# One of GpSimd's six block differences per chunk pair, done by an accumulating DMA inside SBUF

## The chip, the cores and the metric

The kernel runs on one core of one Trainium2 chip. The metric is the device time of one execution in microseconds. Three runs of the kernel before the change gave 461.73, 461.80 and 462.26 us; their median is 461.8 us. A profiled execution of the same kernel took 462.24 us, of which the profile's span covers 460.4 us. Times inside the profile are counted from the start of that span.

## The reference

The kernel computes a compressed interaction network over a batch of 1024 rows, with 64 fields and an embedding of 16. Three layers multiply every field of the input with every field of the running state, contract the products with a weight matrix, and add a bias. Half of each of the first two layers goes to the output and half to the next layer.

```
for i in range(3):
    z = jnp.einsum('bfe,bge->bfge', x0, h).reshape(B, f0 * fh, e)
    y = jnp.einsum('oc,bce->boe', Ws[i], z) + bs[i][None, :, None]
    if i != 2:
        x_i, h = y[:, :64, :], y[:, 64:, :]
    else:
        x_i, h = y, y
    xs.append(x_i)
return jnp.sum(jnp.concatenate(xs, axis=1), axis=2) @ fc_w.T + fc_b
```

All of it is fp32.

## The kernel before, in words

The batch is cut into 32 chunks of 32 rows. A chunk's columns are 32 rows times 16 embedding values, so N = 512. The products of two copies of the input are symmetric, so a chunk needs 16 product tiles of 128 x 512; four of them form a block `z`, 128 x 2048 fp32, 1 MB. Fourteen such blocks live in SBUF, and `take()` and `used()` hand them out and get them back in the order in which they came free.

Six chunks at the head and tail are done plainly. The other 26 form 13 pairs, and a pair (one chunk called `a`, one called `b`) is done with seven block multiplications in place of eight, in the manner of Strassen and Winograd. For that, sums and differences of product blocks and of weight blocks are needed. Per pair:

- VectorE makes the product blocks X (of chunk a), B22, T3 and B21, in two blocks each that the code tells apart by j = 0 and j = 1 (`w_product` L630, printed by the profile as `z<-xa,xp` at L632).
- GpSimd makes six differences, `w_mix` L641, printed as `z<-z,z` at L647. With j = 0 the whole block of four tiles is taken (128x2048), with j = 1 only three of the four (128x1536). The six are, in this order: T2 = T3 - X for j = 0 and j = 1; T3 = B22 - T2 for j = 0 and j = 1, in place; T2 = T2 - B21 for j = 0 and j = 1, in place. The last two are called the final T2 here.
- TensorE multiplies these blocks with weights and with sums of weights (`ws`, of five parts s1, s2, s3, s4 and neg) and collects the results in the PSUM tiles alpha, beta and delta. All of it is printed at L524, the helper `mm`. A weight is 128 x 64, so a multiplication fills half of TensorE's columns; the two halves run side by side.

The weights `ws` are made once at the head by `w_sums` (L774): GpSimd makes s1 to s3, ScalarE writes s4 = -h and neg.

The order is written by hand. Every job is put down with a time, `at(when, ...)`, in units of one slot, and at the end all jobs are issued in the order of these times (L994). The times decide only the order on each engine's queue; what an engine waits for is worked out from the tiles that it reads and writes. `window` (L729) lays out one pair's multiplications as two columns, one for each half of TensorE, and `zipped` interleaves them. The first column has 7 jobs on X, a few that fill up from the pair before, 7 on T2 (`w_run(p, alpha, s2, "T2")`), fill again, and 7 on T3 with s1. The second column has 7 on T3 with s3, 10 left over from the pair before, 7 on B21, and then the jobs on the final T2 (`w_run(p, delta, neg, "T2")`), of which one or two are left to the next pair's window (`second_fill`, L710). So T2 is read twice: first in its first form at jobs 10 to 16 of the first column, then in its final form from job 24 of the second column. The first pair of the 13 differs (L848 to L853): its window has fewer jobs, T2 in its first form is jobs 9 to 15 of the first column, the final T2 starts at place 20 of the second column, where three of the places before it are empty, and one of its B21 blocks is made by GpSimd.

Loads of the next pair are put down by `load_pair` (L755) and issued by SyncE: `xa` (1 MB each, L144), four `xb` of 256 KB (L158), `e` and `xx` (128 KB each, L162 and L167).

In the lists of `make_pair` (L679) the first ten times are those of the products, the six of `mixed` those of the differences: -14, -6.9, 7.2, 12.4, 16.4, 21.7 for the first pair and -5, 2.8, 7.2, 12.4, 16.4, 21.7 for the others.

Of the kernel before, what the change touches and what calls it, by code (L numbers as in the profile page):

```python
# [38 lines left out]
AF = mybir.ActivationFunctionType  # L39
ALU = mybir.AluOpType  # L40
# [10 lines left out]
NI = 4  # L51
# [17 lines left out]
def cin_kernel(ctx, tc, xra, xrb, wh, w0r, w1h, w2t, wx1, wx0, vec, out):  # L69
    nc = tc.nc  # L70
# [8 lines left out]
    def const_tile(name, shape):  # L79
        return const.tile(shape, F32, tag=name, name=name)  # L80

    blocks = [const_tile(f"z{n}", [128, NI, N]) for n in range(NZ)]
    vacant, left = list(range(NZ)), {}

    def take(uses=1):
        n = vacant.pop(0)
        left[n] = uses
        return n

    def used(n, times=1):  # L90
        left[n] -= times
        assert left[n] >= 0
        if left[n] == 0:
            vacant.append(n)
# [22 lines left out]
    for base in (0, 64, -64):  # L117
        nc.gpsimd.affine_select(
            out=shift, in_=shift, compare_op=ALU.not_equal, fill=1.0, base=base,
# [11 lines left out]
    ws = const_tile("ws", [128, 5, 2 * NI, F])  # L131
# [275 lines left out]
    def m_ap(f1, f2, dims):  # L407
        return bass.AP(tensor=md.tensor, offset=md.offset + f1 * row + f2 * F, ap=dims)
# [3 lines left out]
    for half, queue in enumerate((nc.sync, nc.scalar)):  # L412
        queue.dma_start(
            out=m_ap(0, 32 * half, [[row, F], [1, 32 * F]]), in_=m_rows[halves[half]]
# [5 lines left out]
        out=m_ap(64, 68, [[row, 4], [4 * F, 7], [1, 4 * F]]),  # L420
        in_=m_rows[0:4, 4 * F :].rearrange("p (k c) -> p k c", c=4 * F),
# [92 lines left out]
    def at(when, fn, *args, **flags):  # L514
        ops.append((when, len(ops), fn, args, flags))

    def zipped(when, *columns):
        for n, column in enumerate(columns):
            for m, job in enumerate(column):
                if job is not None:  # L520
                    at(when + m + n / len(columns), *job)
# [99 lines left out]
    def w_run(p, out, w, name, start=False, at_t=0, order=GROUPS):  # L621
        return [
            (w_job, p, out, w, j * NI + i + at_t, name, start and n == 0)
            for n, (j, i) in enumerate(order)
        ]

    wh_all, wq_all = w_all[:, :, 0:64], w_all[:, :, 64:128]
    s1, s2, s3, s4, neg = (ws[:, n] for n in range(5))
# [12 lines left out]
    def w_mix(p, j, out, in0, in1):  # L641
        p.setdefault(out, {})
        if j not in p[out]:
            p[out][j] = p["X"][j] if j and p["k"] > 3 else take(9 - 2 * j)
        o, x, y = p[out][j], p[in0][j], p[in1][j]
        tiles = slice(j, NI)
        nc.gpsimd.tensor_tensor(  # L647
            blocks[o][:, tiles], blocks[x][:, tiles], blocks[y][:, tiles], ALU.subtract
        )
        for b in (x, y):  # L650
            if b != o:
                used(b)
# [26 lines left out]
    def make_pair(t, p, when, mixed):  # L679
        a, b = p["a"], p["b"]  # L680
        for when, c, j, name, uses in (
            (when[0], b, 2, "B22", 5), (when[1], b, 0, None, 0), (when[2], b, 0, "T3", 9),
            (when[3], a, 0, "X", 5), (when[4], b, 3, "B22", 6), (when[5], b, 1, None, 0),
            (when[6], b, 1, "T3", 9), (when[7], a, 1, "X", 12 if p["k"] > 3 else 6), (when[8], a, 2, "B21", 5),
            (when[9], a, 3, "B21", 6),
        ):
            if name is None:
                at(t + when, w_both, p, j)
                continue
            if name == "B21" and j == 2 and p["k"] == 3:  # L690
                at(t + when, w_product, p, c, j, name, uses, engine=nc.gpsimd)
                continue
            if name != "T3":
                at(t + when - (3.3 if p["k"] > 4 and name == "B22" and j == 2 else 2.7), second, c, j)
            at(t + when, w_product, p, c, j, name, uses)
        for when, j, *names in zip(
            mixed, (0, 1, 0, 1, 0, 1), *zip(
                *(2 * (("T2", "T3", "X"),) + 2 * (("T3", "B22", "T2"),) + 2 * (("T2", "T2", "B21"),))
            )
        ):  # L700
            at(t + when, w_mix, p, j, *names)

    def first_fill(p):
        a = p["a"]
        return [
            (w_job, p, beta, wq_all, NI, "X"), (w_job, p, beta, wq_all, NT - NI, "B21"),
            (lambda: q_extra(a, va, p["beta"]),),
        ]

    def second_fill(p):  # L710
        return [
            (w_job, p, delta, wh_all, NI, "X"), (w_job, p, delta, wh_all, NT - NI, "B21"),
        ] + w_run(p, delta, neg, "T2")[7 - p["late"] :]

    def left_run(p, out, start=False):
        return [(w_job, p, out, neg, NI, "T3", start), (w_job, p, out, s4, NI, "B22")]
# [1 line left out]
    def late_run(p, left=True):  # L718
        b = p["b"]
        return (left_run(p, alpha) if left else []) + w_run(p, alpha, s4, "B22") + [(lambda: q_extra(b, vb, p["alpha"]),)]  # L720
# [8 lines left out]
    def window(t, p, fill, late, pad=[], order=GROUPS[4:] + GROUPS[:4]):  # L729
        zipped(  # L730
            t,
            w_run(p, alpha, wq_all, "X", True, order=order) + fill[0] + w_run(p, alpha, s2, "T2")
            + fill[1] + w_run(p, alpha, s1, "T3")
            + [(w_job, p, alpha, wh_all, NI, "T3"), (w_job, p, alpha, s1, NI, "B22")],
            w_run(p, delta, s3, "T3", True) + late
            + w_run(p, beta, wq_all, "B21", True, 2 * NI)
            + pad + w_run(p, delta, neg, "T2")[: 7 - p["late"]],
        )
        at(t + 30.2, squares, p)
        at(t + 6.8, snap_p1, p)  # L740
        at(t + 6.9, snap_p7, p)
        at(t + 6.8 + len(fill[0]) + 7, snap_u2, p)

    def end_pair(t, p, whens):
        hb_, qa, uub, ha, uua, xv, add = whens
        at(t + hb_, w_hb, p)
        at(t + qa, w_qa, p)
        at(t + uub, w_uu, p, alpha, "A", snaps[2])
        at(t + ha, w_ha, p)
        at(t + uua, w_uu, p, delta, "O", snaps[0])  # L750
        at(t + xv, x_v0x, p["k"])
        at(t + add, sums, p["k"])


    def load_pair(t, p, b0, a0, b1, a1):  # L755
        a, b = p["a"], p["b"]
        at(t + b0, load_xa, b)
        at(t + b0, load_xb, b, 2, 0)
        at(t + a0, load_xa, a)
        at(t + a0, load_xb, a, 0)  # L760
        at(t + b1, load_xb, b, 3, 1)
        at(t + a1, load_xb, a, 1, 2, 3)
        for c in (b, a):
            at(t + 1, load_e, c)
            at(t + 14, square, c)
        at(t + 1.1, load_xx, p["k"])
# [7 lines left out]
    def w_sums(m):  # L774
        h, q = w_all[:, 8 * m : 8 * m + 8, 0:64], w_all[:, 8 * m : 8 * m + 8, 64:128]
        if m:
            nc.gpsimd.tensor_tensor(ws[:, 3], q, ws[:, 1], ALU.subtract)
            nc.gpsimd.tensor_tensor(vb[halves[1]], va[halves[1]], w0ds[halves[1]], ALU.subtract)
            nc.scalar.activation(ws[:, 4], h, AF.Identity, scale=-1.0)
            nc.scalar.activation(ws[:, 4, NI], ws[:, 2, NI], AF.Identity, scale=-1.0)  # L780
            return
        nc.gpsimd.tensor_tensor(ws[:, 2], h, q, ALU.subtract)
        nc.gpsimd.tensor_tensor(ws[:, 1], ws[:, 0], q, ALU.add)
# [49 lines left out]
    for n in range(NPAIR):  # L833
        k = n + 3
        s = k % 2
        p = {
            "k": k, "A": halves[s], "O": halves[1 - s], "b": 2 * k + s, "a": 2 * k + 1 - s,
            "late": 1 + n % 2 if n else 0,
        }
        pairs.append(p)  # L840
        t = T0 + SPAN * n
        if n == 0:
            load_pair(t, p, -39.9, -33.3, -33.15, -27)
            make_pair(
                t, p, (-23.4, -20.7, -20.4, -17.8, -17.2, -16.8, -16.6, -7, -13.5, 3),
                (-14, -6.9, 7.2, 12.4, 16.4, 21.7),
            )
            left5 = [[(contract_half, 5, 3, i, n) for i in (2, 3)] for n in range(2)]  # L848
            window(
                t, p, ([left5[1][0], (q_extra, 4, va)], [left5[1][1]]),  # L850
                [left5[0][0], (q_extra, 5, va), None, None], [left5[0][1], None],
                GROUPS,
            )  # L853
        else:
            q = pairs[-2]
            load_pair(t, p, -34, -28, -27.8, -27.7)
            make_pair(
                t, p, (-21.4, -18.7, -18.4, -15.8, -12.2, -9.5, -6.1, -2, 1.6, 4.2),
                (-5, 2.8, 7.2, 12.4, 16.4, 21.7),
            )  # L860
            window(t, p, (first_fill(q), second_fill(q)), late_run(q))
            end_pair(t, q, (0.7, 11.7, 17.9, 22.3, 23.2, 24, 27.5))
# [220 lines left out]
```

## Time and profile before

| what | value |
|---|---|
| median of three runs | 461.8 us |
| profiled execution | 462.24 us |
| its span | 460.4 us |
| TensorE's granted clock over the span | 1.00 |
| VectorE busy | 394.0 us, 86% |
| ScalarE busy | 117.1 us, 25% |
| GpSimd busy | 367.7 us, 80% |
| the 78 differences of GpSimd | 310.4 us, 4019 ns each on the mean |
| one difference of 128x2048, of 128x1536 | 4.55 us, 3.46 us |
| one product block on VectorE | 2280 ns |
| DMA, all queues | 86.04 MB, 187 GB/s on the mean |

A group line of the profile gives the line of the program, the engine, the operation, what is written and read, the shapes and the count; then the busy time and the mean duration of one; then the idle time of the engine just before them and what ended most of it. In a timeline line the first number is the start, the second the duration, both in us. PE is TensorE, PEld its weight loads, DVE VectorE, ACT ScalarE, POOL GpSimd and SP SyncE. An fp32 multiplication shows as two instructions.

### The profile page before, as it was taken

How to read it: one execution, taken by the hardware profiler on the slowest of the kernel's cores; microseconds unless marked ns; L12 is line 12 of the kernel's file. 1: busy time of each engine (PE TensorE's matmuls, PEld its weight loads, DVE VectorE, ACT ScalarE, POOL GpSimd, SP SyncE). 2: the span in 40 equal slices, each digit the busy share in tenths (PEclk: the TensorE clock that was granted, in tenths of full speed). 3: DMA queues.
4: the chain of work that ended last, by engine and by line, in shares of the span. 5: the costliest groups of instructions: out<-in, count | busy, mean ns of one | idle time of the engine just before them, and what ended most of it. 6: DMA issues, size and time to landing. Idle time of an engine off the chain costs nothing.

```text
span 460.4 us, 6106 instructions
## 1 busy us (share of the span) xinstructions
PE 453.5 (99%) x2328; PEld 166.5 (36%) x2328; DVE 394.0 (86%) x284; ACT 117.1 (25%) x216; POOL 367.7 (80%) x112
## 2 busy tenths in 40 slices
PE   7999999999999999999999999999999999999997
PEld 4565343343333333333333333333333333333335
DVE  3995599899898989989898998989899998979551
ACT  2162250241313123131213213131311313124011
POOL 5323688998998979899798979989798989989800
DMA  8996998393728173663818264481827448240000
GB/s 295 417 297 149 324 407 321 130 323 111 270 86 319 30 260 140 188 212 131 282 35 290 100 233 166 135 277 48 304 73 250 161 163 279 79 149 18 22 0 2
DMA packets 32613, 86.04 MB, mean 187 GB/s; under 512 B 6116, under 2 KB 6788, under 8 KB 27656
## 3 DMA queue, kind: packets, MB, share of 16 engines
q1 hardware_dynamic: 31800, 84.70, 53.4%
q10 hardware_dynamic: 784, 0.95, 0.8%
q8 instruction: 18, 0.29, 0.3%
q14 instruction: 11, 0.09, 0.1%
HBM read 84.00 MB, written 1.64 MB: 186 GB/s over the span
## 4 chain that ended last, share of the span: by engine, by line
PE 82%; DMA 7%; DVE 3%; SPq 2%; POOL 2%; ACT 1%; issue 1%; POOLq 0%; DVEq 0%
PE alpha L524 57%; PE delta L524 9%; PE beta L524 7%; PE q L524 3%; DMA z<-in_wx 3%; PE acc L250 2%; DMA xa<-in_xra 2%; DVE z L632 2%; DMA xb<-in_xrb 1%; DMA md<-z 1%; SPq L457 1%; POOL z L240 1%; POOL z L535 1%; PE misc L113 1%; PE xp L219 1%
## 5 line engine op out<-in xcount | busy, mean ns | idle before, releaser
L647 POOL TENSOR_TENSOR z<-z,z 128x2048 f32<-128x2048 f32 x78 | 310.4, 4019 | 31.3 <-PE alpha L524 31.3
L632 DVE TENSOR_TENSOR z<-xa,xp 128x2048 f32<-128x2048 f32 x103 | 232.6, 2280 | 16.2 <-POOL z L647 13.1
L524 PE MATMUL alpha<-z,ws 128*64 128x512 f32 x624 | 211.6, 592 | 0.6 <-DVE alpha L943 0.6
L524 PE MATMUL delta<-z,ws 128*64 128x512 f32 x364 | 163.1, 594 | 0.0
L524 PEld LDWEIGHTS alpha<-z,ws 128*64 128x64 f32 x624 | 66.4, 137 | 113.5 <-issue 110.7
L524 PE MATMUL beta<-z,w_all 128*64 128x512 f32 x234 | 105.0, 593 | 0.0
L552 ACT COPY xp<-xb 128x512 f32<-128x512 f32 x88 | 51.6, 588 | 204.8 <-DVE z L632 181.3
L524 PE MATMUL alpha<-z,w_all 128*64 128x512 f32 x208 | 94.2, 595 | 1.1 <-DVE uu L288 0.7
L524 PEld LDWEIGHTS delta<-z,ws 128*64 128x64 f32 x364 | 48.6, 137 | 13.6 <-issue 11.2
L240 DVE TENSOR_TENSOR z<-xa,xp 128x2048 f32<-128x2048 f32 (+2 forms) x23 | 45.1, 2003 | 9.6 <-ACT xp L552 8.2
L524 PEld LDWEIGHTS alpha<-z,w_all 128*64 128x64 f32 x208 | 27.4, 137 | 61.1 <-issue 48.0
L240 POOL TENSOR_TENSOR z<-xa,xb 128x2048 f32<-128x2048 f32 x6 | 27.2, 4557 | 20.6 <-DMA xb<-in_xrb 20.6
L524 PEld LDWEIGHTS beta<-z,w_all 128*64 128x64 f32 x234 | 31.4, 137 | 14.6 <-issue 14.5
L250 PE MATMUL acc<-z,w_all 128*64 128x256 f32 x256 | 29.1, 382 | 1.6 <-DVE z L240 1.4
L524 PE MATMUL acc<-z,w_all 128*64 128x512 f32 (+1 forms) x96 | 30.0, 594 | 0.0
L524 PE MATMUL delta<-z,w_all 128*64 128x512 f32 x52 | 24.6, 593 | 0.0
L250 PEld LDWEIGHTS acc<-z,w_all 128*64 128x64 f32 x256 | 18.0, 137 | 13.8 <-DVE z L240 3.1
L292 DVE TENSOR_REDUCE acc<-uu 128x64 f32<-128x1024 f32 (+2 forms) x19 | 19.6, 1035 | 0.2
L638 DVE TENSOR_TENSOR xp<-xp,xb 128x512 f32<-128x512 f32 x26 | 18.2, 699 | 0.8
L655 ACT COPY snap<-alpha 64x512 f32<-64x512 f32 x13 | 7.6, 581 | 41.7 <-PE delta L524 34.2
L524 PE MATMUL y<-e,v 64*64 64x512 f32 x64 | 17.0, 613 | 0.0
L524 PE MATMUL q<-z,w_all 128*64 128x384 f32 (+1 forms) x128 | 16.9, 381 | 0.0
(117 smaller groups left out, 322.5 us busy)
## 6 DMA issues: line engine op xcount, KB each, us to landing
xa<-in_xra SPq DMA_DIRECT2D x32, 1024.0 KB, 4.7
xb<-in_xrb SPq DMA_DIRECT2D x128, 256.0 KB, 6.8
e<-in_xra SPq DMA_DIRECT2D x28, 128.0 KB, 4.5
xx<-in_xra SPq DMA_DIRECT2D x28, 128.0 KB, 2.5
z<-in_w2t SPq DMA_DIRECT2D x2, 1024.0 KB
z<-in_wx SPq DMA_DIRECT2D x2, 1024.0 KB, 9.2
z<-in_w1h SPq DMA_DIRECT2D x1, 1024.0 KB
xa<-in_xra SPq DMA_DIRECT2D x3, 256.0 KB
```

The source lines that it names most:

```text
L113: nc.tensor.matmul(misc[:, 0:n], zeros, zeros[:, 0:n], start=True, stop=True)
L219: nc.tensor.matmul(xbs[c][j][halves[h]], shift[halves[r], at : at + F], xas[c][halves[r], 0, :], start=True, stop=True,)
L240: engine.tensor_tensor(blocks[zs[c, j]][:, at, :], xas[c][:, at, :], xbs[c][j].unsqueeze(1).to_broadcast([128, last - first, N]), ALU.mult,)
L250: nc.tensor.matmul(accs[c][halves[n]], w_all[:, t, 0:64], blocks[zs[c, j]][:, i, n * H2 : (n + 1) * H2], start=(t == 0), stop=(j == last a ...
L292: nc.vector.tensor_reduce(acc[rows, of, k, half], uu[rows, of if at is None else at, E * half.start : E * half.stop].rearrange("p k (b e) ...
L457: queue.dma_start(out=ms[halves[half], 1, j * NI : (j + 1) * NI], in_=skewed(0, 16 * half + 4 * (j + 1), [[row, NI], [1, F]]),)
L524: nc.tensor.matmul(out, w, rhs, start=start, stop=stop, skip_group_check=True)
L552: nc.scalar.copy(bank, xbs[c][j])
L632: engine.tensor_tensor(blocks[b], xas[c], xbs[c][j].unsqueeze(1).to_broadcast([128, NI, N]), ALU.mult)
L638: nc.vector.tensor_tensor(bank, bank, xbs[p["b"]][j], ALU.add)
L647: nc.gpsimd.tensor_tensor(blocks[o][:, tiles], blocks[x][:, tiles], blocks[y][:, tiles], ALU.subtract)
L655: nc.scalar.copy(snaps[0][p["O"]], alpha(p))
```

## The change

The final T2 of j = 0 is no longer a GpSimd operation. GpSimd issues a DMA that reads block B21 and adds it into block T2, both in SBUF. A DMA of this kind adds[...]. So the signs are turned: T2 is now X - T3, T3 becomes B22 + T2, and the final T2 is T2 + B21. To make up for it, s2 (`ws[:, 1]`), which multiplies the first T2, is negated in place at the head by one more ScalarE instruction, after GpSimd has used the old value for s4's part `ws[:, 3]`; and the final T2 is multiplied with the plain weights `wh_all` (tiles 8 to 15) where it was multiplied with `neg`. The other five differences stay on GpSimd.

The order on GpSimd's queue changes as well. It was: T2 j0, T2 j1, T3 j0, T3 j1, final T2 j0, final T2 j1. Now it is: T2 j0, T2 j1, T3 j0, the DMA for the final T2 j0, T3 j1, final T2 j1. The number of TensorE's and VectorE's instructions and their order stay as they were.

```diff
@@ w_mix
-        nc.gpsimd.tensor_tensor(
-            blocks[o][:, tiles], blocks[x][:, tiles], blocks[y][:, tiles], ALU.subtract
-        )
+        if in1 == "B21" and j == 0:
+            nc.gpsimd.dma_start(out=blocks[o], in_=blocks[y], accum_op=ALU.add)
+        else:
+            nc.gpsimd.tensor_tensor(
+                blocks[o][:, tiles], blocks[x][:, tiles], blocks[y][:, tiles],
+                ALU.subtract if in1 == "T3" else ALU.add,
+            )
@@ make_pair
-                *(2 * (("T2", "T3", "X"),) + 2 * (("T3", "B22", "T2"),) + 2 * (("T2", "T2", "B21"),))
+                *(2 * (("T2", "X", "T3"),) + 2 * (("T3", "B22", "T2"),) + 2 * (("T2", "T2", "B21"),))
+    def p4_run(p):
+        return w_run(p, delta, wh_all, "T2", at_t=2 * NI)
@@ second_fill
-        ] + w_run(p, delta, neg, "T2")[7 - p["late"] :]
+        ] + p4_run(p)[7 - p["late"] :]
@@ window
-            + pad + w_run(p, delta, neg, "T2")[: 7 - p["late"]],
+            + pad + p4_run(p)[: 7 - p["late"]],
@@ w_sums
+            nc.scalar.activation(ws[:, 1], ws[:, 1], AF.Identity, scale=-1.0)
             nc.scalar.activation(ws[:, 4], h, AF.Identity, scale=-1.0)
@@ the times of the differences, first pair and others
-                (-14, -6.9, 7.2, 12.4, 16.4, 21.7),
+                (-14, -6.9, 7.2, 14.2, 14.1, 18),
-                (-5, 2.8, 7.2, 12.4, 16.4, 21.7),
+                (-5, 2.8, 7.2, 14.2, 14.1, 18),
```

## The prediction

> **What bounds the kernel now.** I read the busy shares first, then the chain of work that ended last, then one steady pair on the timeline.
>
> ```profile
> PE 453.5 (99%) x2328; PEld 166.5 (36%) x2328; DVE 394.0 (86%) x284; ACT 117.1 (25%) x216; POOL 367.7 (80%) x112
> PE 82%; DMA 7%; DVE 3%; SPq 2%; POOL 2%; ACT 1%; issue 1%; POOLq 0%; DVEq 0%
> ```
>
> TensorE is busy for 453.5 of 460.4 us and is 82% of the chain; GpSimd is 2% of it. A busy TensorE need not be at its peak, so I looked at its steps. In a steady pair (the window that starts at 244.72) two matmuls, one for each column half, start every 0.43 us without a hole. The change leaves their number alone, so there is nothing to win there. Time can only be lost, where a block comes too late for TensorE. The block in question is the final T2 of j = 0. GpSimd makes it now:
>
> ```profile
> 251.02 4.56 POOL L647 TENSOR_TENSOR z<-z,z 128x2048 f32<-128x2048 f32 x1
> 255.54 3.48 POOL L647 TENSOR_TENSOR z<-z,z 128x1536 f32<-128x1536 f32 x1
> 258.97 4.55 POOL L647 TENSOR_TENSOR z<-z,z 128x2048 f32<-128x2048 f32 x1
> 263.49 3.44 POOL L647 TENSOR_TENSOR z<-z,z 128x1536 f32<-128x1536 f32 x1
> ```
>
> These are T3 j0, T3 j1, final T2 j0, final T2 j1. TensorE's rows on both sides:
>
> ```profile
> 252.92 0.59 PE L524 MATMUL beta<-e,va 128*64 128x512 f32 x1
> ...
> 264.95 0.59 PE L524 MATMUL beta<-z,w_all 128*64 128x512 f32 x1
> 265.37 0.59 PE L524 MATMUL alpha<-z,ws 128*64 128x512 f32 x1
> 265.38 0.59 PE L524 MATMUL delta<-z,ws 128*64 128x512 f32 x1
> ```
>
> The first row ends the fill ahead of the T2 jobs. T2 j0's eight instructions follow at 0.4265 us each, so the last starts at 252.92 + 8 x 0.4265 = 256.33 and ends at 256.92: only then may T2 j0 be overwritten. The last row is the first reader of the final T2. The **budget in a steady pair** is 265.33 - 256.97 = 8.4 us (0.04 us off each end for the signal). GpSimd's own version ends at 263.52, 1.9 us early.
>
> The first pair is tighter:
>
> ```profile
> 97.85 0.59 PE L524 MATMUL alpha<-z,ws 128*64 128x512 f32 x1
> 100.42 4.54 POOL L647 TENSOR_TENSOR z<-z,z 128x2048 f32<-128x2048 f32 x1
> 103.62 1.88 PE L524 MATMUL alpha<-z,ws 128*64 128x512 f32 x4
> 105.01 0.64 PE L524 MATMUL delta<-z,ws 128*64 128x512 f32 x1
> ```
>
> T2 j0 is released at 97.85 + 0.59 = 98.44. GpSimd finished the final T2 at 104.96 and TensorE took it at 105.01, 0.1 us after its previous matmul (104.91). The **budget in the first pair** is 104.92 - 98.48 = 6.4 us, with no slack at all.
>
> Last, the DMA engines in the two budgets (the last two numbers of a row are DMA share and GB/s):
>
> ```profile
> 257.00:265.40 8.40, 8.40 (x42) 2.76 (x40) 8.18 (x9) 1.87 (x3) 8.40 (x3) 1.00 0.07 23
> 98.00:100.00 2.00, 2.00 (x13) 0.67 (x9) 1.97 (x2) 0.00 (x0) 2.00 (x1) 1.00 0.97 409
> 100.00:102.00 2.00, 1.99 (x10) 0.61 (x9) 2.00 (x2) 0.92 (x2) 2.00 (x2) 1.00 1.05 340
> 102.00:104.00 2.00, 2.00 (x9) 0.70 (x9) 2.00 (x2) 0.96 (x3) 2.00 (x1) 1.00 0.85 164
> ```
>
> and the page's row of a plain 1 MB load (issue to landing, us):
>
> ```profile
> xa<-in_xra SPq DMA_DIRECT2D x32, 1024.0 KB, 4.7
> ```
>
> In the steady pair they stand idle just then; in the first pair loads fill them until 104.
>
> [...]
>
> **The change, part by part.**
>
> *The transfer in a steady pair.* No row of before shows an adding transfer. `xa` moves as many bytes: at the 409 GB/s of the full engines 1.049 MB takes 2.56 us, so 4.7 - 2.56 = 2.1 us are fixed. [...] Lower end, the add at a copy's rate: 2.5 + 2.56 = 5.1 us. Upper end, two reads and the write one after the other: 2.5 + 3 x 2.56 = 10.2. I take two reads with the write beside them: 2.5 + 5.1 = 7.6 us, and 0.3 us for a 128 KB `e` load that shares the stretch (131 KB / 409): 7.9. That is under 8.4 with 0.5 us to spare: hidden, 12 pairs, 0 us. If the cover is gone, every us of lateness costs 12 us.
>
> *The transfer in the first pair.* The loads after 98.5 are 409 x 1.5 + 340 x 2 + 164 x 2 = 1.62 MB. [...] I take the middle, **2.7 us, once**.
>
> *GpSimd's queue.* The DMA instruction stands ahead of T3 j1 and waits for TensorE. In the steady pair GpSimd is free at 255.58, waits until 256.97[...], so T3 j1 runs 258.0 to 261.5 in place of 255.5 to 259.0. Its reader comes after the four T3 j0 jobs that start at 262.79, at 266.2: 4.7 us of cover. Final T2 j1 then ends at 265.0, where it ended at 266.93; its reader is at 265.38 + 4 x 0.853 = 268.8. In the first pair T3 j1 ends at about 103, its reader is at 105.34 + delay. 0 us. GpSimd saves 3.5 us a pair off the path.
>
> *VectorE.* The block B21 j0 comes free only when the transfer lands, and a later product takes it. In a steady pair that product starts 23.8 us into the window (242.40 - 218.6), the landing is at 20.6: 0. In the first pair it is the product at 107.83, which would slip to 109.1; the X product that follows ends 2 x 2.28 later, at 113.7, and TensorE, 2.7 us late, wants it at 114.9. 0.
>
> *ScalarE at the head.* One more 128x512 pass, 0.63 us by L779, and the group now waits for GpSimd's L777 (ends 58.0; L779 began at 58.06 anyway). The copy behind it slips by 0.6 us, VectorE's next product by 0.2; VectorE then waits 0.58 us for GpSimd at 80.14. 0; without that cover, 0.2.
>
> *Weights `wh_all` for `neg`:* same shapes, 0.
>
> Sum: 462.24 + 2.7 = 464.9 for an execution like the profiled one, which lies 0.44 above the median; on the median 461.8 + 2.7 = **464.5 us**.
>
> **The rivals.** (1) *The transfer is late in every pair.* For it: only 0.5 us of slack on an operation no row shows. At the upper end, 10.5 us with the `e` load, it costs 12 x 2.1 = 25 us; half-way, 12 x 1.0 + 3.5 = 15.5, so **477**. It decides from 8.4 us on. (2) *No change, the other side:* in the first pair the sum lands within 6.4 us. That needs an add at a copy's rate which gets past the loads[...]; **462.0**. Against it: the second read. (3) *Faster, a freer GpSimd speeds VectorE.* TensorE starts every second window 0.11 us late on a VectorE product that ends at 244.67; six of these are 0.7 us, so at best **461.1**, within 0.2%. Against it: VectorE's product takes 2.28 us with GpSimd busy or idle beside it. That the change doesn't do what it says can be left out: the built order of instructions shows 13 DMAs in place of 13 differences.
>
> **Numbers.** 0.2% (0.9 us) is about what a measurement of this kernel can tell from no change. Chances: forecast 0.42, (1) 0.37, (2) 0.16, (3) 0.05. Of these, slower by over 0.2% are nearly all of the first two, 0.79; same 0.17; faster 0.04. The forecast's own range is 463.0 to 466.5 (1.2 to 4.2 late). The range 461.8 to 484 leaves out the faster case, part of (2), and the worst of (1).
>
> **What would show it.** Right: TensorE's one new hole near 105, 1 to 4 us, ended by a DMA `z<-z`; none in later pairs; landing about 8 us after the issue. Wrong: a hole at the same place of every window (rival 1), or none (rival 2). GpSimd should fall to about 367.7 - 13 x 3.5 = 322 us. An adding transfer slower than two reads would break the forecast most.

## The result and the profile after

The changed kernel takes 468.8 us where the kernel before takes 462.0 on the same chip: a ratio of 1.0147 with a 95% interval of [1.0130, 1.0165], so 6.8 us more. The forecast was 464.5. The profiled execution of the changed kernel took 468.71 us, with a span of 466.9.

The page of the changed kernel: busy times, the clock granted to TensorE in 40 slices, the software queue (the one that GpSimd's DMA uses: packets, MB, share of 16 engines), the chain of work, GpSimd's group of differences, and the row of the adding transfer (KB each, us from issue to landing).

```profile
PE 455.7 (98%) x2328; PEld 166.7 (36%) x2328; DVE 393.8 (84%) x284; ACT 117.4 (25%) x217; POOL 321.7 (69%) x112
PEclk9999999997999999999999999999999999999999
q0 software_dynamic: 1872, 13.63, 15.1%
PE 78%; DMA 12%; SPq 3%; DVE 2%; issue 1%; ACT 1%; POOL 1%; POOLq 0%; DVEq 0%; ACTq 0%
L650 POOL TENSOR_TENSOR z<-z,z 128x1536 f32<-128x1536 f32 (+1 forms) x65 | 256.3, 3960 | 58.5 <-PE alpha L524 57.4
z<-z POOLq DMA_DIRECT2D x13, 1024.0 KB, 7.5
```

GpSimd is 46 us less busy, as meant, and a landing takes 7.5 us. TensorE has as many instructions as before (2328) and yet 2.2 us more busy time: some of them ran slower, in the one slice where the clock shows a 7. The waits of TensorE in the changed kernel (total us, times, longest) name one transfer, and VectorE waits once for the same one:

```profile
PE delta L524 <- DMA z<-z: 5.0, 1, 5.0
...
DVE z L632 <- DMA z<-z: 2.9, 1, 2.9
```

The place, from the changed kernel's chain of waits between 96 and 120 us (start, us, what; POOLq is the part of GpSimd that issues):

```profile
97.09 0.02 issue
97.11 0.02 POOLq L648
97.13 0.54 issue
97.67 11.44 DMA z<-z
109.11 0.04 issue
109.15 1.11 PE delta L524
...
110.27 0.85 PE delta L524
...
113.69 0.62 PE delta L524
...
114.31 0.43 PE delta L524
```

This is the first pair. T2 j0 comes free at 97.11, GpSimd's DMA starts 0.56 us later, the sum lands after 11.44 us and TensorE takes it 0.04 us after that. Then five of its steps of two matmuls take 0.85 us or more, and a sixth 0.62, where a step takes 0.43. The granted clock over one-us stretches of the changed kernel says why. (A row gives the stretch, its length, the busy us of PE, PEld, DVE, ACT and POOL, then the clock, the DMA share and GB/s.)

```profile
106.00:107.00 1.00, 0.00 (x0) 0.00 (x0) 0.35 (x1) 0.00 (x0) 1.00 (x1) 1.00 1.06 221
107.00:108.00 1.00, 0.00 (x0) 0.00 (x0) 0.00 (x0) 0.00 (x0) 1.00 (x1) 0.56 0.53 107
113.00:114.00 1.00, 1.00 (x4) 0.24 (x2) 0.71 (x1) 0.25 (x1) 0.00 (x0) 0.53 0.99 410
114.00:115.00 1.00, 1.00 (x7) 0.28 (x4) 0.00 (x0) 0.34 (x1) 0.00 (x0) 1.00 1.08 418
```

The one-us stretches between the second row and the third stand at 0.50. So the clock is halved from 107.12 (0.88 us of the second row) to 113.94 (0.94 us of the third row): 6.8 us, of which TensorE works from 109.15 on, 4.8 us at half speed, 2.4 lost.

The steady pairs are clean. From the changed kernel's timeline:

```profile
210.72 0.86 POOL L648 DMA_DIRECT2D z<-z  x1 [1.92 <-issue]
...
218.61 0.59 PE L524 MATMUL delta<-z,w_all 128*64 128x512 f32 x1
```

That transfer landed at 218.20, 7.48 us after its issue and 0.41 us before its first reader. Over the twelve steady pairs the room is 0.22 to 0.46 us.

**The sum.** From the first matmul of the first pair's window to the start of the window two pairs on, by the timelines: 138.53 - 87.07 = 51.46 us before, 144.86 - 85.70 = 59.16 after. That is 7.7 us: the step with the hole is 5.61 us in place of 0.43 (5.2), and the slow steps are 2.4 to 2.6. The rest of the program up to the end is 0.2 us longer. In this execution the head was 1.4 us sooner (85.70 against 87.07), so that the spans differ by 6.5 only. All seven profiled executions with the changed head have this start between 85.7 and 86.4; of the kernel before there is one profile, so that I can't tell the difference from chance. The first experiment, which has the same head, shows no gain.

### The profile page after: what moved, and what is told of

The parts are those of the page before. It is cut to its first block, busy times and chain, and to the rows that moved or that the text cites. A ratio compares the mean times of both kernels' runs of the same rounds, so it can differ in the third digit from the quotient of the medians.

```text
span 466.9 us, 6113 instructions
## 1 busy us (share of the span) xinstructions
PE 455.7 (98%) x2328; PEld 166.7 (36%) x2328; DVE 393.8 (84%) x284; ACT 117.4 (25%) x217; POOL 321.7 (69%) x112
## 3 DMA queue, kind: packets, MB, share of 16 engines
q0 software_dynamic: 1872, 13.63, 15.1%
## 4 chain that ended last, share of the span: by engine, by line
PE 78%; DMA 12%; SPq 3%; DVE 2%; issue 1%; ACT 1%; POOL 1%; POOLq 0%; DVEq 0%; ACTq 0%
PE alpha L524 56%; PE delta L524 11%; PE beta L524 7%; DMA xb<-in_xrb 4%; PE q L524 3%; DMA z<-in_wx 3%; DMA z<-z 2%; DMA xa<-in_xra 2%; DMA md<-z 1%; SPq L457 1%; POOL z L535 1%; DVE z L240 1%; SPq L144 1%; DVE shift L539 0%; DVE z L632 0%
## 5 line engine op out<-in xcount | busy, mean ns | idle before, releaser
L650 POOL TENSOR_TENSOR z<-z,z 128x1536 f32<-128x1536 f32 (+1 forms) x65 | 256.3, 3960 | 58.5 <-PE alpha L524 57.4
L524 PE MATMUL alpha<-z,ws 128*64 128x512 f32 x624 | 214.2, 596 | 0.6 <-DVE alpha L951 0.6
L524 PE MATMUL delta<-z,w_all 128*64 128x512 f32 x234 | 107.3, 604 | 5.0 <-DMA z<-z 5.0
L524 PEld LDWEIGHTS alpha<-z,ws 128*64 128x64 f32 x624 | 66.8, 138 | 111.8 <-issue 109.8
L524 PE MATMUL delta<-z,ws 128*64 128x512 f32 x182 | 80.9, 596 | 0.0
L240 DVE TENSOR_TENSOR z<-xa,xp 128x2048 f32<-128x2048 f32 (+2 forms) x23 | 45.1, 2002 | 9.4 <-ACT xp L552 9.0
L524 PEld LDWEIGHTS delta<-z,w_all 128*64 128x64 f32 x234 | 32.4, 139 | 35.9 <-issue 29.8
L240 POOL TENSOR_TENSOR z<-xa,xb 128x2048 f32<-128x2048 f32 x6 | 27.2, 4559 | 20.1 <-DMA xb<-in_xrb 20.1
L250 PE MATMUL acc<-z,w_all 128*64 128x256 f32 x256 | 29.1, 382 | 1.0 <-DVE z L240 0.8
L648 POOL DMA_DIRECT2D z<-z x13 | 11.5, 882 | 25.0 <-issue 23.0
L524 PEld LDWEIGHTS delta<-z,ws 128*64 128x64 f32 x182 | 23.9, 137 | 1.6 <-DVE uu L288 0.5
L250 PEld LDWEIGHTS acc<-z,w_all 128*64 128x64 f32 x256 | 18.0, 137 | 13.3 <-DVE z L240 2.5
L669 DVE SCALAR_TENSOR_TENSOR snap<-alpha,vs,snap 64x512 f32<-64x512 f32 x13 | 9.8, 751 | 10.0 <-PE y L524 9.7
```

Source lines behind the costliest of these rows:

```text
L240: engine.tensor_tensor(blocks[zs[c, j]][:, at, :], xas[c][:, at, :], xbs[c][j].unsqueeze(1).to_broadcast([128, last - first, N]), ALU.mult,)
L250: nc.tensor.matmul(accs[c][halves[n]], w_all[:, t, 0:64], blocks[zs[c, j]][:, i, n * H2 : (n + 1) * H2], start=(t == 0), stop=(j == last a ...
L524: nc.tensor.matmul(out, w, rhs, start=start, stop=stop, skip_group_check=True)
L648: nc.gpsimd.dma_start(out=blocks[o], in_=blocks[y], accum_op=ALU.add)
L650: nc.gpsimd.tensor_tensor(blocks[o][:, tiles], blocks[x][:, tiles], blocks[y][:, tiles], ALU.subtract if in1 == "T3" else ALU.add,)
L669: nc.vector.scalar_tensor_tensor(hb_, alpha(p), bh1[p["A"]], hb_, ALU.add, ALU.add)
```

## The experiments

Each kernel is set against executions of the kernel before on the same chip: 461.11 us for "the loads held back" and "the steady transfer issued later", 461.46 us for the other four.

**Theory.** The whole loss is made in the first pair: its transfer is held up by loads that are ahead of it on the same DMA engines, so TensorE stands idle, and the idle time then costs TensorE its clock. **Rivals.** The loss is spread over the pairs (waits that the profile hides, a poorer interleave, the changed order on GpSimd); or the first transfer is slow for a reason of its own, such as being the first of its kind, and not for the loads; or the low clock is not a consequence of the hole.

### The first pair's sum left on GpSimd

```diff
-        if in1 == "B21" and j == 0:
+        if in1 == "B21" and j == 0 and p["k"] > 3:
...
-                (-14, -6.9, 7.2, 14.2, 14.1, 18),     # the first pair's times
+                (-14, -6.9, 7.2, 12.4, 16.4, 21.7),
```

> First pair as before (GpSimd's addition, old order), the adding transfer kept in the other twelve pairs. Theory A (all of the loss is the first pair's: a hole of about 5.2 us in TensorE and about 2.6 us of half clock behind it; in the other pairs the transfer is hidden): 462.0 us, within 0.6 us of the kernel before, no hole at the first pair, landing 7.5 us after the issue in the twelve. Rival B (the twelve pairs lose something too, by traffic or by a blocked GpSimd queue): 463.5 to 467 us.

Measured: 461.76 us against 461.46, ratio 1.0002 [0.9993, 1.0011]. The page and the waits of TensorE in this kernel:

```profile
PE 452.7 (99%) x2328; PEld 166.6 (36%) x2328; DVE 394.2 (86%) x284; ACT 117.5 (26%) x217; POOL 325.4 (71%) x112
z<-z POOLq DMA_DIRECT2D x12, 1024.0 KB, 7.5
```
```profile
PE acc L250 <- DVE z L240: 1.2, 1, 1.2
PE alpha L524 <- DVE z L632: 0.8, 1, 0.8
```

No transfer ends a wait of TensorE, and the steady windows are as long as before: the same matmul comes back after 26.06 and 27.03 us by turns in both kernels. Twelve transfers, the turned signs, the extra ScalarE instruction and the new weights together cost nothing that the runs can tell (0.3 us, within the interval). They gain nothing either, though GpSimd is 42 us less busy. The twelve landings took 7.4 to 7.9 us, the longest being the first, so a first transfer outside the loads is hardly slow.

### Only the first pair's sum by the transfer

```diff
-        if in1 == "B21" and j == 0:
+        if in1 == "B21" and j == 0 and p["k"] == 3:
...
-                (-5, 2.8, 7.2, 14.2, 14.1, 18),       # the other pairs' times
+                (-5, 2.8, 7.2, 12.4, 16.4, 21.7),
```

> The adding transfer in the first pair alone; the other twelve pairs have GpSimd's addition in the old order. Theory A: the whole loss comes back, 468.8 us (467.5 to 470), with a hole of about 5 us and slow steps behind it. Rival B: less than the whole loss, 463 to 467 us.

Measured: 468.31 us against 461.46, ratio 1.0156 [1.0136, 1.0175]. One transfer brings back the whole loss, so the spread-out rival is out. Its landing took 10.5 us. TensorE's wait for it, and the clock behind that, in this kernel (waits, then one-us stretches):

```profile
PE delta L524 <- DMA z<-z: 4.1, 1, 4.1
```
```profile
108.00:109.00 1.00, 0.57 (x4) 0.29 (x6) 0.50 (x1) 0.00 (x0) 1.00 (x1) 1.00 0.00 0
109.00:110.00 1.00, 1.00 (x6) 0.29 (x4) 1.00 (x1) 0.00 (x0) 1.00 (x1) 0.59 0.09 16
...
112.00:113.00 1.00, 1.00 (x6) 0.39 (x4) 0.99 (x1) 0.00 (x0) 0.00 (x0) 0.70 0.70 262
```

TensorE is back at 108.42, still at full clock, and the clock falls after that, at 109.18, until 112.60 (0.50 in both rows between 110 and 112): 3.4 us at half speed, 1.7 lost. Its first two windows are 6.0 us longer than before: 4.1 + 1.7 and 0.2 over. The profiled execution took 467.20 us with a mean granted clock of 0.996; the other three took 468.25 to 469.61 with 0.992 or 0.993, which is about twice as much time at half clock. So the price of the clock differs from one execution of the same kernel to the next.

### The loads held back

One small read of T2 j0, put on SyncE's queue ahead of the loads, makes the queue wait until the sum is there. All work is done.

```diff
+    def hold_loads(p):
+        nc.sync.dma_start(
+            out=m_ap(0, 0, [[F, 1], [1, 16]]), in_=blocks[p["T2"][0]][0:1, 0, 0:16]
+        )
...
+            at(t + 14.15, hold_loads, p)              # first pair only
```

> The changed kernel with one 64-byte store put on SyncE's queue behind the first pair's adding transfer, from the block that the transfer writes; so the loads of a later pair (xa 1 MB, xb 0.5 MB, e and xx 0.5 MB) wait until it has landed. Theory A (the first pair's landing takes 10.5 to 11.4 us and not 7.5 because loads fill the engines): landing 7.5 to 8.7 us after the issue, hole 1.7 to 3 us, 464 to 466 us. Rival B (it is slow because it is the first of its kind, or for another reason of the first pair): landing 10.5 to 11.4 us, 468 us.

Measured: 463.57 us against 461.11, ratio 1.0056 [1.0037, 1.0075]. The first landing falls from 11.4 to 8.1 us and TensorE's wait from 5.0 to 1.7:

```profile
PE delta L524 <- DMA z<-z: 1.7, 1, 1.7
```

The time was expected at 464 to 466 us. The loads were the cause of the late landing, of 3.4 us out of the 4.0 by which it lay above the steady 7.5; the last 0.6 stays unexplained. How they do it shows in the DMA view by queue (packets, MB, share of 16 engines). In the changed kernel, whose DMA was issued at 97.67, in two-us stretches from 100, 102, 104, 106 and 108, q1 being the loads and q0 the sum:

```profile
q1 hardware_dynamic: 205, 0.34, 108.3%
...
q0 software_dynamic: 34, 0.28, 66.8%
q1 hardware_dynamic: 133, 0.20, 48.2%
...
q0 software_dynamic: 53, 0.43, 104.2%
...
q0 software_dynamic: 50, 0.33, 79.4%
...
q0 software_dynamic: 7, 0.01, 2.4%
```

With the loads held and the issue at 98.01, in stretches from 98, 100, 102 and 104:

```profile
q0 software_dynamic: 16, 0.13, 32.2%
...
q0 software_dynamic: 48, 0.39, 97.7%
...
q0 software_dynamic: 54, 0.44, 108.9%
...
q0 software_dynamic: 26, 0.08, 21.2%
```

The sum's own packets take 5.1 us of all sixteen engines in the first list (the shares of q0 times two us) and 5.2 in the second. In the changed kernel none is seen before 102.2, 4.5 us after the issue; with the loads held the first comes 1.6 us after it, and in a steady pair 1.4. All these loads had been issued by 97.1, ahead of the sum. So the sum did not share the engines with the loads from the start. For about 3 us it came behind those already queued; what holds it back inside the engines the trace does not show.

Even unhindered it is late here: the first pair's budget is 6.4 us and the transfer needs 8.1 + 0.6, so that TensorE waits 1.7 us. Of the 2.5 us that this kernel loses, the first two windows hold 2.0 (53.43 against 51.46), and a later window whose transfer took 8.2 us to land is 0.3 longer.

### A copy in place of the sum

```diff
-            nc.gpsimd.dma_start(out=blocks[o], in_=blocks[y], accum_op=ALU.add)
+            nc.gpsimd.dma_start(out=blocks[o], in_=blocks[y])
```

> The transfer copies B21 over T2 instead of adding it; the addition is left out, so the final T2 of j = 0 is B21. Theory A (the add's second read sets the data time: 646 ns for an 8 KB packet against 309 for a copy, eight packets per engine): landing 4.8 us after the issue in the twelve pairs in place of 7.5, first pair's landing 2 to 4 us earlier, hole 1.5 to 3.5 us, clock drop smaller or absent: 463.5 to 466 us. Rival (the software queue itself is slow, add or not): landing 7.5 us and 468.8 us.

The addition is left out here. Measured: 466.63 us against 461.46, ratio 1.0120 [1.0092, 1.0147]. From the page of this kernel, its waits, and its clock in one-us stretches:

```profile
q0 software_dynamic: 1872, 13.63, 8.3%
z<-z POOLq DMA_DIRECT2D x13, 1024.0 KB, 4.9
```
```profile
PE delta L524 <- DMA z<-z: 2.5, 1, 2.5
```
```profile
106.00:107.00 1.00, 0.00 (x0) 0.00 (x0) 0.72 (x2) 0.00 (x0) 1.00 (x1) 0.98 0.02 8
107.00:108.00 1.00, 0.94 (x4) 0.32 (x6) 0.86 (x1) 0.00 (x0) 1.00 (x1) 0.50 0.00 0
...
110.00:111.00 1.00, 1.00 (x6) 0.25 (x4) 1.00 (x1) 0.05 (x1) 0.32 (x1) 0.81 0.69 180
```

The same bytes take 8.3% of the engines in place of 15.1%: over the 1664 large packets a sum's packet is 0.151 x 16 x 466.9 / 1664 = 0.68 us, a copy's 0.083 x 16 x 464.0 / 1664 = 0.37, a factor of 1.83. The steady landing is 2.6 us shorter. The addition is a price of the transfer, but not the reason for the first pair's lateness: the copy lands 8.9 us after its issue there, 4.0 above its own median, just as the sum is 4.0 above. The time came out a little above what was expected (463.5 to 466): a hole of 2.5 us sufficed to halve the clock for 3.4 us (106.96 to 110.38).

### The hole filled with idle matmuls

Six matmuls of zeros stand ahead of the first reader in the first pair; all work is done.

```diff
+        jobs = w_run(p, delta, wh_all, "T2", at_t=2 * NI)
+        return [(filled, p, jobs[0])] + jobs[1:] if p["k"] == 3 else jobs
+    def filled(p, job):
+        for n in range(6):
+            mm(delta(p), wh_all[:, 0], nc.const_aps.tensor(0.0, [128, N]))
+        job[0](*job[1:])
```

> The changed kernel with six more matmuls of zeros (two instructions each, 12 x 0.427 = 5.1 us) on delta ahead of the first reader of the first pair's final T2, so that TensorE works while it would wait. They add zero to the result. Theory A1 (the slow steps behind the hole are TensorE's clock, lowered because it stood idle): full clock throughout, 466.2 us (465.5 to 467). Rival A2 (the slow steps come from something else, such as data traffic or the weights): slow steps stay, 468.8 us.

Measured: 467.24 us, ratio 1.013 [1.011, 1.015]. The landing is as late as in the changed kernel (11.2 us), the hole left is 1.3 us, and the clock stays up. From this kernel's page and waits:

```profile
PEclk9999999999999999999999999999999999999999
```
```profile
PE delta L524 <- DMA z<-z: 1.3, 1, 1.3
```

All four executions have a mean granted clock of 1.000, where those of the changed kernel have 0.992 to 0.996. The first two windows lose 5.1 us where the changed kernel loses 7.7, so the low clock is a consequence of the hole and costs 2.6 us; filling it leaves the lateness. Over the whole kernel, each against its own before, only 1.0 us of that shows (5.8 lost in place of 6.8; 466.2 us was expected). In this profile two later stretches from one transfer's issue to the next are 0.5 and 0.4 us longer than in the changed kernel, at 27.43 and 26.56 us; their transfers took 8.3 us to land, which is over the room. Why they did is open.

### The steady transfer issued one GpSimd operation later

The first pair stays on GpSimd as in the first experiment, and in the others the DMA stands behind T3 j1 and not ahead of it.

```diff
-                (-5, 2.8, 7.2, 14.2, 14.1, 18),       # the other pairs' times
+                (-5, 2.8, 7.2, 14.0, 14.1, 18),
```

> First pair on GpSimd as in e1; in the other twelve pairs the adding transfer is put behind T3 j1 on GpSimd's queue, so it is issued 1.5 to 2.1 us later, when T3 j1 ends. Theory A (in a steady pair the landing has only some 0.35 us to spare before TensorE wants the block): 1.3 to 1.7 us late in each of twelve pairs, 477 to 482 us if holes this short leave TensorE's clock alone, up to 500 us if each lowers it. Rival B (the steady pairs have room of 2 us or more): 461.5 to 462.5 us.

Measured: 475.85 us against 461.11, ratio 1.0321 [1.0300, 1.0341]: 14.7 us, 1.2 per pair on the mean. The landing takes as long as ever (7.4 us; 9.0 in the first of the twelve). TensorE's waits for a transfer are 1.8 us in all, 1.6 of them for that first one, so the loss must be looked for elsewhere. The timeline of this kernel:

```profile
209.85 0.83 POOL L648 DMA_DIRECT2D z<-z  x1
...
216.26 1.02 PE L524 MATMUL alpha<-z,ws 128*64 128x512 f32 x2
217.30 0.64 PE L524 MATMUL delta<-z,w_all 128*64 128x512 f32 x1
217.30 0.64 PE L524 MATMUL alpha<-z,ws 128*64 128x512 f32 x1
```

From 216.26 one half of the columns works alone; the other waits for the landing at 217.25. TensorE counts as busy all that time. The DMA goes out 6.4 us ahead of its first reader's turn at 216.27, where the changed kernel leaves 7.9 (210.72 to 218.61): 1.5 us later, which uses up the room and leaves the block 1.0 us late. The expectation had 1.3 to 1.7 us and so 477 to 482. This is the prediction's first rival, made true by 1.5 us of delay.

## Why the prediction was wrong in size

- **TensorE as the bound, GpSimd's saving worth nothing:** right. GpSimd went to 321.7 us (322 forecast), and with the first pair left alone the time is that of before (461.76 against 461.46).
- **The transfer in a steady pair:** right. From the release to the landing 0.56 + 7.48 = 8.04 us, forecast 7.9; the addition costs 2.6 us over a copy, forecast 2.56 as a second read. That it is a read was assumed: the runs show a sum's packet at 1.83 times a copy's (0.68 and 0.37 us), not what the time goes into. The forecast's fixed part of 2.5 us lies above the 2.1 read from `xa`, and no trace of before showed that much; the copy's 4.9 us leave 4.9 - 2.56 = 2.3. That the forecast comes so near is in part luck: the sum's packets took 5.5 us and not 5.1 (72.9% of the 7.48 us from issue to landing), which the 0.3 us set aside for the `e` load covered. The room is 0.2 to 0.5 us, and 1.2 us per pair are due as soon as the issue slips by one operation.
- **GpSimd's queue, VectorE, ScalarE at the head, the weights:** each was put at 0, and outside the first pair they sum to 0 by the first experiment. GpSimd's next operation begins 0.6 us after the DMA's start in a steady pair (210.72 to 211.33), where the forecast's times leave 1.0 (256.97 to 258.0). VectorE's product in the first pair waited 2.9 us for the landing where 1.3 were foreseen; no wait of TensorE followed from it.
- **The step that failed: "The transfer in the first pair", with "I take the middle, 2.7 us, once".** The place was right and the term was mis-sized, in two ways. First, it took the middle of two ends: 4.2 us late, with the sum sharing the engines with the loads from its start, and 1.2, with the sum ahead of them. Both ends, with the times of the first byte and the last in them, were assumptions that no trace of before showed. The sum came behind the loads that were queued, and TensorE lost 5.2. From 102 to 104 both queues move (66.8% and 48.2% of the engines), but in the 4.5 us before 102.2 no packet of the sum is seen. There was no reason in the profile to go below the late end: a DMA share of 0.97 to 1.05 until 102 spoke for it.
- **The term that was missing, the second way:** TensorE's clock after a hole, 2.4 to 2.6 us. The hole was forecast, what TensorE does behind a hole was not, and the profile before has no case of it: TensorE's longest wait there is 1.4 us (`PE acc L250 <- DVE z L240: 1.4, 1, 1.4`). In the runs here the granted clock fell to 0.50 in or after holes of 2.5, 4.1 and 5.0 us (below).
- **Two figures of the prediction have no working that holds:** 461.8 + 4.2 is 466.0, not the 466.5 at which its own range ends, and the 3.5 us in the half-way case of the first rival stand underived. Neither changes the outcome.

Together 5.2 + 2.4 to 2.6 make up the 7.7 us of the first two windows. The medians show 6.8; the head, 1.4 us sooner in the profiled execution, may be the difference, which one profile of each can't settle.

## What to carry to other kernels

Cost a transfer put in place of an engine's operation in the stage with the least room, and there against the loads that are already queued when it starts: the steady stage hid twelve of these and gained nothing by them, and the one in the first stage cost 6.8 us. Where the bound is TensorE, a hole can have two prices, its length and the clock behind it (5.2 and 2.4 to 2.6 us in the changed kernel); for the holes of 1.3 to 1.7 us here only the first was due. In the last experiment the waits that kept half of the columns empty were not in the list of waits (1.8 us there, 14.7 us lost): look for lone halves on the timeline.

## What the runs showed that I had not expected

The half-clock stretches are 6.82 us (107.12 to 113.94) in the changed kernel, 3.42 us with only the first pair changed (109.18 to 112.60) and 3.42 us with the copy (106.96 to 110.38): 3.42 us twice and about double that once, behind holes of 4.1, 2.5 and 5.0 us. The fall did not keep to one place in the hole either. It came 3.0 us after the hole began in the changed kernel (104.13 to 107.12), 2.4 us after it with the copy (104.53 to 106.96), and with only the first pair changed not until TensorE had been at work again for 0.8 us (108.42 to 109.18). What sets the moment of the fall, or the length of the stretch, the traces do not show. Holes of 1.3 to 1.7 us in three other kernels dropped nothing: the mean granted clock of their profiled executions is 0.999 to 1.000, as before. Nothing was measured between 1.7 and 2.5 us, and whether the length of the hole alone decides was not tried.
